# A two-layer decoder on one core: scatters of routed rows and fills of empty rows, moved to other slots of a written-out plan

## The chip, the cores and the metric

The kernel runs on one core of a Trainium2 chip, in float32. The time is the device time of one execution in microseconds; the median of several runs is compared. A separate execution, taken with the hardware profiler, gives the profile.

## The reference

The input x has 32 batch rows of 128 tokens with 128 features; a context has 32 rows of 128 tokens with 96 features, and a mask marks some of its tokens. Six residual blocks follow each other, each with a layer norm in front:

```python
x = x + rope_attention(ln(x))                    # 16 heads of 8
x = x + cross_attention(ln(x), ctx)              # 16 heads of 8
x = x + gated_moe(ln(x))                         # 8 experts, best 2, and 2 shared ones
x = x + causal_attention(ln(x))                  # 16 heads of 8, rotated q and k
x = x + latent_attention(ctx, ln(x), mask)       # 2 heads of 64, keys from ctx and x
x = x + relu_moe(ln(x))                          # 8 experts of width 512, best 2, biases
```

The last block matters most here. For each token it takes the softmax of eight router logits, keeps the two largest, divides them by their sum, and adds the two experts' outputs with these weights:

```python
probs = softmax(x @ router_w + router_b)
w, i = top_k(probs, 2); w = w / sum(w)
out = sum over the two: w * (relu(x @ w1[i] + b1[i]) @ w2[i] + b2[i])
```

## The kernel before

**Groups, slots and phases.** The 32 batch rows form 8 groups of 4. The kernel is one plan written by hand: `at(slot, phase, fn)` puts a function that issues instructions into a slot and a phase of it, and the slots are run through in order, so that each engine's queue has its instructions in the order of the plan. The phases that matter here are, in order, "open", "pre", (the attention's own work), "inner", "mid" and "post". The three attentions take 64 slots each (0–63 rope, 64–127 cross, 128–191 causal), two slots for each batch row; after slot 191 the plan goes on with latent attention, routing and experts. `done(stage, g)` is 8·(8·stage + g) + 17, the slot in which group g has left that attention; `done(2, 7)` is 201.

**Routing.** For the last block the groups are routed in five units, `UNITS = [(0, 1), (2, 3), (4, 5), (6,), (7,)]`: three pairs and two single groups. The units are collected into three parts, `UNITS_OF = [(0, 1), (2,), (3, 4)]`, so that groups 0–3, 4–5 and 6–7 go through the experts one part after the other. `plan_route` (from L1590) plans a unit: the norm's statistics (L1612, L1613 on DVE), its scale `r_rs` (L1618–L1621, on POOL), the normed rows (`rows`, L1629 on ACT, L1634 on POOL), the turned rows, logits (L1653), the choice of two experts, and then in one "mid" phase `ranks`: the gates' weights (`r_e`), a matmul that counts how many tokens before each chose the same expert (`ranks_pe`, L1701–L1703), and `places` (L1707–L1725). `places` is eleven small DVE instructions and two small POOL copies for a unit. It makes of the counts the row number at which each token goes into a buffer in DRAM (`r_ati`), the counts carried to the next unit (`carry`, L1713), and two extra columns of each row: the weight (L1724) and the token's number (L1725).

**Scatter.** Each expert has a region in the DRAM buffer `slots[f]` of its part f. `scatter(c, k)` (L1729) is one indirect DMA issued by POOL. It writes the 128 tokens of one batch row k, for their c-th choice, as rows of 130 floats (520 bytes) to the places in `r_ati`. A pair of groups has 16 such scatters, a single group 8: 64 in all. The plan places two per slot, one "pre" and one "inner", from the slot behind `ranks` on: a pair's 16 in 8 slots, a single group's 8 in 4 slots. The slots are 184–191, 200–207 and 216–223 for the pairs, and 222–225 and 230–233 for the single groups.

**Empty rows.** Rows of `slots` that no token goes to must hold something harmless. `preset(n)` (L2054–L2058) fills a quarter of one part's buffer with the row `nowhere`, whose token number is out of range, so that its result is not stored. There are 12 presets, issued by SP: four of 2210 KB and eight of 1170 KB, 18.2 MB. `once` (L2079) plans them in slots 4, 8, ... 48. The other loads and stores of these stages go through SP's queue too: the writes of `kv` (L1043, one per group), the copies of x to DRAM (`held`, L364), and for the first block of experts the gates' round trip through DRAM (`spread`, written at L918, read back by two DMAs per group as `g` at L921, which POOL waits for in `h`, L941).

**Experts.** `expert_blocks` (from L1818) works on blocks of 128 rows of `slots[f]`, two blocks (a pair) per slot. A part has 39, 23 and 23 blocks. For a pair: `fetch` loads two blocks of rows (`bx`, L1868, by SP, 20 buffers), `weights` copies the experts' weights (`w`, L1877 on ACT, L1879 on DVE), `turn` transposes the rows on PE (L1887, then `bxT` L1889 on DVE), `hidden` is the first product (L1897 on PE) with bias and relu (`bh`: L1903 on ACT, L1905 on DVE), `result` the second (L1914) with the gate's weight (`bo`: L1921 on ACT, L1923 on DVE), and `leave` stores each block's 128 results by an indirect DMA of POOL to the rows of `y` (L1928). So POOL issues two indirect DMAs per slot for the experts, and those of the scatters beside them. At the end `gather` and `finish` read `y` back and add it to x.

**When a part begins.** `beside` (from L1957) sets the slots in which the parts begin:

```python
begins = [done(2, 3) + 40]
begins.append(max(begins[0] + (NB[0] + 1) // 2, done(2, 5) + 40))
begins.append(max(begins[1] + (NB[1] + 1) // 2, done(2, 7) + 33))
```

These are 209, 229 and 241. A part's first four pairs are fetched in the "post" phase of that slot; its table of blocks is made four slots before. The first fetch of a part waits until all scatters into its buffer have landed.

Of the kernel before, what the change touches and what calls it, by code (L numbers as in the profile page):

```python
# [37 lines left out]
NB = [2 * r // BLOCK + E - 1 for r in ROOM]  # L38
# [75 lines left out]
def decoder(ctx: ExitStack, tc: tile.TileContext, a: dict, out: bass.AP):  # L114
# [132 lines left out]
    def wide(t, shape, axis):  # L247
        return t.unsqueeze(axis).to_broadcast(shape)
# [9 lines left out]
    def folded_bias(w_o, b_v, row, t):  # L258

        ps = bank(ps_m)  # L260
        nc.tensor.matmul(ps[:, :D], b_v.to_broadcast([D, P]), w_o, start=True, stop=True)
        nc.vector.tensor_tensor(t, ps[:, :D], row, ALU.add)
# [1304 lines left out]
    def store(g):  # L1567
        nc.sync.dma_start(out[g * NG : (g + 1) * NG].rearrange("b p d -> p b d"), X[g])
# [10 lines left out]
    def router(slots, lazy):  # L1579
# [8 lines left out]
        def plan_route(at, g, t):  # L1588
# [5 lines left out]
            groups = UNITS[q]  # L1594
# [5 lines left out]
            def tile8(tag, dtype=F32):  # L1600
                return small.tile([P, N2, E], dtype, tag="r8_" + tag, name="r8_" + tag, bufs=2)[:, :n2, :]
# [87 lines left out]
            def gates():  # L1689
                e, w = m["e"], col8("w")  # L1690
                nc.vector.tensor_tensor(e, e, m["both"], ALU.mult)
                nc.vector.tensor_reduce(w, e, AX.X, ALU.add)
                nc.vector.reciprocal(w, w)
                nc.vector.tensor_tensor(e, e, wide(w, [P, n2, E], 2), ALU.mult)
# [13 lines left out]
            def places():  # L1708
                place = tile8("place")
                nc.vector.tensor_tensor(  # L1710
                    place, m["rp"][:, : n2 * E].rearrange("p (b e) -> p b e", e=E), wide(before, [P, n2, E], 1), ALU.add
                )
                nc.vector.tensor_tensor(carry[q], m["rp"][:, n2 * E : (n2 + 1) * E], before, ALU.add)  # L1713
                at2 = small.tile([P, 2, N2], F32, tag="r_at", name="r_at", bufs=2)
                for c in range(2):
                    t = tile8("t")
                    nc.vector.tensor_tensor(t, m["picks"][:, c], place, ALU.mult)
                    nc.vector.tensor_reduce(at2[:, c, :n2], t, AX.X, ALU.add)
                m["ati"] = small.tile([P, 2, N2], I32, tag="r_ati", name="r_ati", bufs=2)
                nc.vector.tensor_copy(m["ati"][:, :, :n2], at2[:, :, :n2])  # L1720
                for c in range(2):
                    t = tile8("t")
                    nc.vector.tensor_tensor(t, m["picks"][:, c], m["e"], ALU.mult)
                    nc.vector.tensor_reduce(m["rows"][c][:, :n2, D + 1], t, AX.X, ALU.add)  # L1724
                    nc.gpsimd.tensor_copy(m["rows"][c][:, :n2, D].bitcast(I32), token[:, c, NG * groups[0] : NG * groups[0] + n2])  # L1725

            def scatter(c, n):
                def fn():
                    ins = nc.gpsimd.indirect_dma_start(  # L1729
                        slots[f], bass.IndirectOffsetOnAxis(ap=m["ati"][:, c, n : n + 1], axis=0), m["rows"][c][:, n, :], None,  # L1730
                        bounds_check=SLOTS[f] - 1, oob_is_err=False,
                    )
                    tc.declare_no_dep(ins.ins, group=f"slots{f}", reason="no two tokens have one slot")
                    tc.add_to_no_dep_group(f"slots{f}", ins.ins)
                return fn
# [34 lines left out]
            def ranks():  # L1770
                gates()
                ranks_pe()
                places()

            def gates_over(u):
                def fn():
# [27 lines left out]
            if len(groups) > 1:  # L1804
                t += 1
            at(t + 6, "mid", choose3)
            at(t + 7, "mid", ranks)
            n = 0
            for k in range(n2):
                for c in range(2):  # L1810
                    at(t + 8 + n // 2, ("pre", "inner")[n % 2], scatter(c, k))
                    n += 1
            for u in us:
                at(t + 8 + u, "mid", gates_over(u))
# [138 lines left out]
    def experts(halves, lazy, heads, late):  # L1953

        def beside(at, done):
            def swap():
                heads.close()  # L1957
                lazy["blocks"] = late.enter_context(tc.tile_pool(name="blocks", bufs=3, reuse_waits="tile"))

            def keep(e):  # L1960
                def fn():
                    rows = a["w_f"][e * P : (e + 1) * P]
                    if e == 0:
                        for tag, n in (("w1", W1), ("w2", 512)):
                            lazy[tag] = lazy["blocks"].tile([P, E * n], F32, tag=tag, name="all_" + tag, bufs=1)
                    nc.sync.dma_start(lazy["w1"][:, e * W1 : (e + 1) * W1], rows[:, :W1])
                    nc.sync.dma_start(lazy["w2"][:, e * 512 : (e + 1) * 512], rows[:, W1:])
                return fn

            at(done(2, G - 1) + 2, "open", swap)  # L1970
            for e in range(E):
                at(done(2, G - 1) + 2 + e, "open", keep(e))
            begins = [done(2, 3) + 40]
            begins.append(max(begins[0] + (NB[0] + 1) // 2, done(2, 5) + 40))
            begins.append(max(begins[1] + (NB[1] + 1) // 2, done(2, 7) + 33))

            def plan_part(f):
                table, fetch, weights, turn, hidden, result, leave, gather, finish = halves[f]
                t = begins[f]
                pairs = (NB[f] + 1) // 2  # L1980
                at(t - 4, "mid", table)
                for i in range(4):
                    at(t, "post", lambda i=i: fetch(i))
                for i in range(2):
                    at(t + i, "post", lambda i=i: weights(i))
                at(t + 1, "post", lambda: turn(0))
                for i in range(pairs):
                    s = t + 2 + i
                    if i + 1 < pairs:
                        at(s, "pre", lambda i=i: turn(i + 1))  # L1990
                    at(s, "inner", lambda i=i: hidden(i))
                    at(s + 1, "post", lambda i=i: result(i))
                    at(s + 2, "mid", lambda i=i: leave(i))
                    if i + 4 < pairs:
                        at(s, "post", lambda i=i: fetch(i + 4))
                    if i + 2 < pairs:
                        at(s, "post", lambda i=i: weights(i + 2))
                if f + 1 < len(PARTS):
                    for n, g in enumerate(PARTS[f]):
                        at(begins[f + 1] + 6 + 2 * n, "post", lambda g=g: gather(g))  # L2000
                        at(begins[f + 1] + 8 + 2 * n, "post", lambda g=g: finish(g))
                        at(begins[f + 1] + 10 + 2 * n, "post", lambda g=g: store(g))

            for f in range(len(PARTS)):
                plan_part(f)
        return beside
# [46 lines left out]
    def preset(n):  # L2053

        chunks = SLOTS[n // 4] // (2 * P)
        part = slots[n // 4].rearrange("(c p r) w -> p c (r w)", p=P, r=2)[:, n % 4 * chunks // 4 : (n % 4 + 1) * chunks // 4]
        nc.sync.dma_start(
            part, nowhere.rearrange("p r w -> p (r w)").unsqueeze(1).to_broadcast([P, chunks // 4, 2 * ROW])  # L2058
        )

    def once(at, done):

        at(-8, "mid", lambda: folded_bias(w_o0, b_v0, b_o0, bias0))
        at(8, "mid", lambda: nc.gpsimd.memset(z_all, 0.0))
        at(8, "mid", fold_context)
        at(9, "mid", fold_small)
        at(40, "mid", lambda: folded_bias(w_xo0, b_xv0, b_xo0, biasx))
        at(41, "mid", lambda: masked_bias(b_mx, b_xqk0[:, 0:1], b_xqk0[:, 1:2]))
        for n in range(2):
            at(104 + n, "mid", lambda n=n: fold_rotation(2 * n))  # L2070
        at(106, "mid", lambda: masked_bias(b_m1, b_qk1[:, 0:1], b_qk1[:, 2:3]))
        at(107, "mid", lambda: folded_bias(w_o1, b_v1, b_o1, bias1))
        at(108, "mid", lambda: folded_bias(w_xo1, b_vl, b_xo1, bias_l))
        for n in range(4 * len(PARTS)):
            at(4 + 4 * n, "mid", lambda n=n: preset(n))
        guard = []
        at(138, "mid", lambda: guard.append(cross_guard(word)))
        at(140, "mid", lambda: guard[0]())
# [125 lines left out]
```

## Time and profile before

| | before |
|---|---|
| runs | 1178.01, 1179.47, 1180.0 us |
| median | 1179.47 us |
| the profiled execution | 1184.79 us |
| its span in the profile | 1183.1 us |
| mean granted clock of TensorE | 0.943 |
| busy: PE / DVE / POOL / ACT | 1067.5 / 823.1 / 645.3 / 615.8 us |
| share of the chain that ended last: PE / DVE / POOL / ACT / DMA | 52 / 19 / 10 / 7 / 4% |
| 64 scatters L1729, busy on POOL | 63.6 us |
| 85 stores L1928, busy on POOL | 85.3 us |

How to read it: the engines are PE (matrix products), PEld (its weight loads), DVE, ACT, POOL and SP (which issues DMAs only). The profile cuts the span into 40 equal slices of 29.6 us and gives each engine's busy share in tenths, with a 9 for 90% or more; PEclk is the clock that PE was granted, in tenths. A group of instructions is a line such as "L1729 POOL DMA_INDIRECT slots<-rows,r_ati x64 | busy us, mean ns | idle before it, and what ended most of that idle time": the line of the kernel, the engine, the operation, what it writes and reads, and how often. "remote" and "issue" are names for idle time whose end no event in the trace explains. In a timeline, a bracket behind a row holds the idle time just before it and what ended it. The chain is the work that ended last, followed backwards from the last instruction to whatever released each step.

In the trace the experts' first rows (L1868) are loaded at 917 us and the last store of results (L1928) is issued at 1166 us.

### The profile page before, as it was taken

The numbers are of one execution on the slowest core, as the hardware profiler recorded it, in microseconds if no ns is written. First come the engines' busy times: TensorE is split into PE (matmuls) and PEld (weight loads), VectorE is DVE, ScalarE is ACT, GpSimd is POOL, SyncE is SP. The second block draws the span as 40 slices with busy tenths as digits, with TensorE's granted clock in tenths as the row PEclk, the third lists the DMA queues.
The fourth block names the chain that finished last, engine by engine and source line by source line (L and its number), as shares of the span: only waits on it lengthen the run. The fifth ranks groups of instructions, "written<-read, shape, count | busy, mean of one in ns | idle before, by whom it ended". The sixth has DMA issues, their size and how long they took to land.

```text
span 1183.1 us, 32419 instructions
## 1 busy us (share of the span) xinstructions
PE 1067.5 (90%) x12495; PEld 829.2 (70%) x12495; DVE 823.1 (70%) x2424; ACT 615.8 (52%) x1440; POOL 645.3 (55%) x918
## 2 busy tenths in 40 slices
PE   6999999999999999999998999989988888788893
PEld 3666667677767776677667677767766778678893
DVE  4678878878778666867787788778666565454652
ACT  2356555676655555554555666744633543333551
POOL 4576656434442544235647675746837245555653
PEclk9999989999999999999999999989976899888997
DMA  8753331000121011110110000001115222123432
GB/s 204 220 154 101 101 100 61 29 29 29 38 47 46 7 41 37 38 26 14 38 46 7 11 15 15 16 11 35 31 37 157 69 56 58 38 66 86 107 109 77
DMA packets 77858, 71.24 MB, mean 60 GB/s; under 512 B 14554, under 2 KB 66829, under 8 KB 77696
## 3 DMA queue, kind: packets, MB, share of 16 engines
q1 hardware_dynamic: 72640, 60.08, 18.7%
q0 software_dynamic: 4768, 8.47, 2.1%
q8 instruction: 102, 1.67, 0.6%
q10 hardware_dynamic: 288, 0.52, 0.1%
q14 instruction: 60, 0.49, 0.1%
HBM read 33.39 MB, written 37.02 MB: 60 GB/s over the span
## 4 chain that ended last, share of the span: by engine, by line
PE 52%; DVE 19%; POOL 10%; ACT 7%; issue 6%; DMA 4%; SPq 0%; another core or an unknown queue 0%; DVEq 0%; POOLq 0%; ACTq 0%
PE bank L633 11%; PE bank L1897 5%; PE bank L661 5%; PE bank L1914 5%; DVE msc L636 5%; PE bank L950 3%; DMA g<-spread 3%; POOL h L941 2%; ACT e L644 2%; PE bank L1121 2%; PE bank L511 1%; PE bank L932 1%; DVE qa L540 1%; PE bank L1200 1%; PE bank L1226 1%
## 5 line engine op out<-in xcount | busy, mean ns | idle before, releaser
L644 ACT ACTIVATE e<-bank 128x512 f32<-128x512 f32 x384 | 207.6, 593 | 178.5 <-PE bank L633 174.2
L636 DVE TENSOR_REDUCE msc<-bank 128x4 f32<-128x512 f32 x384 | 245.2, 680 | 70.1 <-PE bank L633 67.1
L633 PE MATMUL bank<-kb,qz 32*128 32x256 f32 x1536 | 243.8, 410 | 12.3 <-DVE msc L636 10.5
L633 PE MATMUL bank<-qa,kb 32*128 32x128 f32 x3072 | 235.9, 289 | 4.5 <-ACT e L644 4.5
L633 PEld LDWEIGHTS bank<-qa,kb 32*128 32x128 f32 x3072 | 196.6, 191 | 9.7 <-ACT e L644 8.8
L633 PEld LDWEIGHTS bank<-kb,qz 32*128 32x128 f32 x1536 | 146.8, 190 | 65.1 <-DVE msc L636 33.2
L1928 POOL DMA_INDIRECT y<-bo,bx x85 | 85.3, 1004 | 81.5 <-ACT bo L1921 44.0
L647 POOL TENSOR_SCALAR_AFFINE_SELECT e<-e 128x512 f32<-128x512 f32 x128 | 79.2, 642 | 69.5 <-ACT e L644 69.2
L661 PE MATMUL bank<-e,vt 128*32 128x128 f32 x3072 | 109.3, 284 | 0.5 <-POOL e L647 0.5
L1897 PE MATMUL bank<-bxT,w 128*128 128x128 f32 x680 | 92.1, 287 | 9.9 <-issue 9.4
L1897 PEld LDWEIGHTS bank<-bxT,w 128*128 128x128 f32 x680 | 85.9, 202 | 12.5 <-issue 12.0
L1914 PE MATMUL bank<-all_w,bh 128*128 x680 | 91.3, 289 | 3.6 <-issue 3.5
L661 PEld LDWEIGHTS bank<-e,vt 128*32 128x32 f32 x3072 | 81.5, 113 | 15.7 <-POOL e L647 1.5
L1914 PEld LDWEIGHTS bank<-all_w,bh 128*128 128x128 f32 x680 | 85.6, 204 | 6.0 <-issue 5.7
L1729 POOL DMA_INDIRECT slots<-rows,r_ati x64 | 63.6, 994 | 34.0 <-issue 18.4
L1905 DVE TENSOR_SCALAR bh<-bank,w 128x128 f32<-128x128 f32 x164 | 46.1, 343 | 43.8 <-remote 19.6
L941 POOL TENSOR_TENSOR h<-h,g 128x512 f32<-128x512 f32 x30 | 38.7, 1298 | 68.9 <-DMA g<-spread 58.3
L338 ACT ACTIVATE xn<-x,ln_nb,ln_rs 128x128 f32<-128x128 f32 x96 | 42.0, 492 | 49.9 <-POOL ln_nb L332 49.3
L1903 ACT ACTIVATE bh<-bank,w 128x128 f32<-128x128 f32 x176 | 50.3, 368 | 19.9 <-remote 7.7
L1207 ACT ACTIVATE le<-bank,lmx 128x256 f32<-128x256 f32 x64 | 26.9, 471 | 64.7 <-DVE lmx L1206 60.3
L540 DVE SCALAR_TENSOR_TENSOR qa<-bank,head_rows,qz 128x128 f32<-128x128 f32 x192 | 57.6, 342 | 0.0
L1921 ACT ACTIVATE bo<-bank,bx 128x128 f32<-128x128 f32 x44 | 16.2, 368 | 76.2 <-PE bank L1914 47.8
(337 smaller groups left out, 2320.5 us busy)
## 6 DMA issues: line engine op xcount, KB each, us to landing
slots<-nowhere SPq DMA_DIRECT2D x8, 1170.0 KB
slots<-nowhere SPq DMA_DIRECT2D x4, 2210.0 KB
g<-spread SPq DMA_DIRECT2D x16, 512.0 KB
bx<-slots SPq DMA_DIRECT2D x85, 65.0 KB
kv<-kcv SPq DMA_DIRECT2D x8, 516.0 KB
lkv<-kv SPq DMA_DIRECT2D x32, 129.0 KB
yg<-y SPq DMA_DIRECT2D x14, 256.0 KB
all_w<-in_w_f SPq DMA_DIRECT2D x8, 258.0 KB
```

The costliest lines, as they stand in the source:

```text
L540: nc.vector.scalar_tensor_tensor(s["qa"][:, u, :], s["mp"], head_rows[:, 1 - u : 2 - u], m["qz"][:, u, i * P : (i + 1) * P], ALU.mult, ALU.add
L633: nc.tensor.matmul(o, l, r, start=start, stop=stop, skip_group_check=True)
L636: nc.vector.tensor_reduce(tops(MSC[bb % 4], 2 * h + j), sc[j].rearrange("p (s n k) -> p s n k", s=2, n=2), AX.X, ALU.max, negate=True)
L644: nc.scalar.activation(e.rearrange("p n q -> p (n q)"), tr[j], AF.Exp, scale=SCALE)
L647: nc.gpsimd.affine_select(out=e, in_=e, compare_op=ALU.is_ge, fill=0.0, base=0, pattern=[[0, 4], [1, P]], channel_multiplier=-1)
L661: nc.tensor.matmul(s3["av"][32 * n : 32 * n + 32, h3 * P : (h3 + 1) * P], m3["vt"][:, i3, h3, n, u, :], es[u][:, n, :], start=(h3 == 0 and ...
L941: engine.tensor_tensor(m["h"][:, c, :], m["h"][:, c, :], m["g"][:, c, :], ALU.mult)
L1729: ins = nc.gpsimd.indirect_dma_start(slots[f], bass.IndirectOffsetOnAxis(ap=m["ati"][:, c, n : n + 1], axis=0), m["rows"][c][:, n, :], Non ...
L1897: nc.tensor.matmul(ps[:, c * P : (c + 1) * P], w[:, c * P : (c + 1) * P], s["xT"][:, u * P : (u + 1) * P], start=True, stop=True)
L1903: nc.scalar.activation(h, p, AF.Relu, bias=bias)
L1914: nc.tensor.matmul(ps[:, u * P : (u + 1) * P], s["h"][:, u, c, :], lazy["w2"][:, bass.ds(at_w + c * P, P)], start=(c == 0), stop=(c == 3),)
L1928: ins = nc.gpsimd.indirect_dma_start(y, bass.IndirectOffsetOnAxis(ap=x[:, D : D + 1].bitcast(U32), axis=0), s["o"][:, u, :], None, bounds_ ...
```

## The change

There are three edits, and a fourth that follows from them.

1. For a pair of groups, `places` is taken out of `ranks` and planned in the next slot's "pre" phase. The pair's 16 scatters begin one slot later, still two per slot: 185–192, 201–208 and 217–224. For a single group `places` stays where it is.
2. For a single group, the 8 scatters are planned one per slot, all in "pre": 222–229 and 230–237 instead of 222–225 and 230–233.
3. The 12 presets are planned in slots 20, 28, ... 108 ("post") instead of 4, 8, ... 48 ("mid").
4. In the third term of `begins`, 33 becomes 37. In both kernels the other term of that maximum is larger (229 + 12 = 241), so the parts begin in the same slots.

No instruction is added or removed.

```diff
             def ranks():
                 gates()
                 ranks_pe()
-                places()
+                if len(groups) == 1:
+                    places()
...
             at(t + 7, "mid", ranks)
+            if len(groups) > 1:
+                at(t + 8, "pre", places)
             n = 0
             for k in range(n2):
                 for c in range(2):
-                    at(t + 8 + n // 2, ("pre", "inner")[n % 2], scatter(c, k))
+                    if len(groups) > 1:
+                        at(t + 9 + n // 2, ("pre", "inner")[n % 2], scatter(c, k))
+                    else:
+                        at(t + 8 + n, "pre", scatter(c, k))
                     n += 1
...
-            begins.append(max(begins[1] + (NB[1] + 1) // 2, done(2, 7) + 33))
+            begins.append(max(begins[1] + (NB[1] + 1) // 2, done(2, 7) + 37))
...
         for n in range(4 * len(PARTS)):
-            at(4 + 4 * n, "mid", lambda n=n: preset(n))
+            at(20 + 8 * n, "post", lambda n=n: preset(n))
```

On the engines' queues this does the following. PE's and ACT's order is the same in both kernels. On DVE only the three pairs' `places` move: in units 0 and 1 behind the latent attention's copy `leT` (L1216), the norm statistics of another group (L1612, L1613) and the product `lqk` (L1122); in unit 2 behind `leT`, the statistics and the experts' `bo` (L1923) and `w` (L1879). On POOL the scatters move: in unit 1 two of them from behind `r_rs` to ahead of it, in unit 2 two from ahead of it to behind it, and the single groups' scatters from two behind each two `leave` stores to one. On SP the presets move: eight stand one by one among the writes of `kv` and the copies `held`, and the last four just before the copies `held` of the fourth to seventh groups, three of them right behind a group's two loads of `g`.

## The prediction, made before the changed kernel ran

> **What bounds the kernel.** I read the page's slices first (forty, each 29.6 us), then the chain of waits, then the timelines of PE and POOL in the last 240 us, where most of what the change moves lies.
>
> ```profile
> PE   6999999999999999999998999989988888788893
> POOL 4576656434442544235647675746837245555653
> PEclk9999989999999999999999999989976899888997
> DMA  8753331000121011110110000001115222123432
> ```
>
> PE is busy nine tenths up to 800 us and holds 52% of the chain. From slice 33 (976 us) on it sags to 8, with a 7 at slice 36 (1065 us), and in slices 31 to 36 the granted clock sags too. That stretch is the expert stage, where scatters of the last units (L1729) stand on POOL beside the expert blocks' leaving rows (L1928):
>
> ```profile
> L1928 POOL DMA_INDIRECT y<-bo,bx x85 | 85.3, 1004 | 81.5 <-ACT bo L1921 44.0
> L1729 POOL DMA_INDIRECT slots<-rows,r_ati x64 | 63.6, 994 | 34.0 <-issue 18.4
> L1905 DVE TENSOR_SCALAR bh<-bank,w 128x128 f32<-128x128 f32 x164 | 46.1, 343 | 43.8 <-remote 19.6
> ```
>
> An indirect DMA takes POOL 0.97 us and 0.30 us of issue behind it: 1.275 us back to back. The windows of ten (columns: busy us and count of PE, PEld, DVE, ACT, POOL, then granted clock, DMA share, GB/s) show what happens where POOL has many in a row:
>
> ```profile
> 1000.00:1010.00 10.00, 9.66 (x87) 9.29 (x87) 8.48 (x36) 6.06 (x16) 5.43 (x6) 1.00 0.23 57
> 1010.00:1020.00 10.00, 6.34 (x36) 4.63 (x35) 0.46 (x2) 1.14 (x4) 7.57 (x9) 0.90 0.18 53
> 1020.00:1030.00 10.00, 7.16 (x35) 6.20 (x36) 5.14 (x21) 2.70 (x8) 3.66 (x5) 0.59 0.07 22
> ```
>
> From 1006.88 to 1023.17 POOL issues 13 indirect DMAs without a break. Six microseconds in, PE falls from 87 matmuls per 10 us to 36, DVE and ACT nearly stop, and none of them names a releaser. The timelines of DVE, ACT and PE:
>
> ```profile
> 1019.78 1.12 DVE L1905 TENSOR_SCALAR bh<-bank,w 128x128 f32<-128x128 f32 x4 [9.54 <-remote]
> 1025.63 0.37 ACT L1921 ACTIVATE bo<-bank,bx 128x128 f32<-128x128 f32 x1 [9.72 <-remote]
> 1016.17 0.27 PE L1887 MATMUL bank<-ident,bx 128*128 128x128 f32 x1 [0.45 <-issue]
> ```
>
> PE then steps singly, one matmul per 0.72 us, until 1025.4. The same follows two more runs: 8 indirect DMAs with two copies (1031.6 to 1042.4: PE gaps of 4.6 us from 1037.7) and 10 (1060.1 to 1072.6: gaps of 2.73, 0.38 and 1.04 us, and ACT's bo 8.87 us late). Runs of 4 with a break of 1.8 us (988 to 1001) leave PE 96% busy, and runs of 2 (1084 to 1150) leave it full at 3.79 us per pair of blocks. So I read: **a run of indirect DMAs longer than about 6 us stalls the other engines until one or two microseconds after its end.** From 1000 to 1084 us PE finishes 12 pairs; at 3.79 us, with 5.7 us of other PE work there, that is 51.2 us, and with the clock's sag it took 79: some 28 us are at stake.
>
> **The change, part by part.** I made the sum against the profiled execution's own 1184.8 us (span 1183.1); the median of the runs is 1179.5, 5.3 less, and I take the difference over unchanged. In the built programs PE and ACT keep their order; the pairs' places move on DVE, and scatters and presets move on POOL and SP.
>
> *Presets* (the empty rows, twelve DMAs on SP). They start at 41 us before, five in a row, and at about 96 us after, one per eight slots, the last at some 415 us:
>
> ```profile
> slots<-nowhere SPq DMA_DIRECT2D x8, 1170.0 KB
> slots<-nowhere SPq DMA_DIRECT2D x4, 2210.0 KB
> ```
>
> Before, they flood the DMA engines (slices 1 to 4), yet a group of the first attention takes 28.45 us under the flood (48.38 to 76.83) and 28.45 us after it (88.73 to 117.18): nothing to win. After, each goes ahead of a write of kv (first read at 619 us), ahead of a held copy, or behind the two loads of g (groups 0 to 2). POOL's h waits for g (58.3 us in all), but on SP the preset stands behind those loads; a held copy of 256 KB already follows there, and the waits with and without one are alike (6.99 to 8.40 us). Cost 0; the bound above is a third of a preset's transfer at the 220 GB/s of slice 1 (5.3 us / 3) on each of three groups, about +6; below 0.
>
> *Pairs.* The places are eleven small DVE instructions, 2.1 us (876.0 to 878.0 in unit 1). A slot later they stand behind leT, lqk and the norm's sums, which PE waits for: 0.66 and 0.79 us at 796 and 798 us (unit 0), 0.82 and 0.76 us near 880 (unit 1). Half of each is gained: −0.7 and −0.8; ends 0 and −1.5 each. What is late next are the scatters, one slot: in unit 1, two of them (2.55 us) move ahead of POOL's r_rs, which ACT's rows (L1629) and PE's L1641 already wait for (1.07 and 0.99 us): +1.3, ends 0 and +2.2. In unit 2, two scatters move from ahead of r_rs to behind it, so the four-long run at 965.6, with ACT's rgT 3.57 us late, starts earlier: −1.5, ends 0 and −4. Sum −1.7.
>
> *Single groups.* Scatters go from two per slot in 222–225 and 230–233 to one in 222–229 and 230–237. In slots 222–223, where unit 2's pair scatters overlap (and, after, 224), POOL's list turns from "y y s s s s" to "y y s s s". By the rows' times that makes the 13-run a 12-run: −1.3. Behind r_rs the list was y y s s, copy, y y, copy, y y; it becomes y y s, copy, y y s, copy, y y s: nine instead of eight: +1.3. The 10-run at 1060 (s s y y s s y y s s) becomes s y y s y y s y y, eight or nine, and the stall behind it halves (8.3 us by the ACT and PE waits, PE's half of it counted): −3.5. The scatters moved out of it go to slots 234–237 with three indirect DMAs each: POOL 3.83 us per slot against PE's 3.79: +1.2, ends +0.2 and +5. Sum −2.3. The lower end: POOL holds 45 indirect DMAs between 1001.4 and 1084, 57.4 us, with 4 us of copies and small operations; if nothing stalls, 61.4 instead of 82.8: −21.
>
> *Part 1's first load* waits on SP for the last scatter of unit 3, before at 1035.7 with the load at 1037.4; PE wants it at 1061.1. After, that scatter sits at slot 229, about 1052.4 by the y y of 1049.9 ahead of it. It lands 2.1 us later (a piece of the chain shows 2.11), and the load needs about 2.8: 1057.3. Cover shrinks from 20 us to 4. Cost 0; +3 if POOL lags. Queued behind that load on SP are only the next loads. The start slots of the parts stay 209, 229 and 241 (33 to 37 is covered by the larger term).
>
> Sum: 0 − 1.7 − 2.3 + 0 = **−4.0 us: 1180.8 by the profile, 1175.5 by the median.**
>
> A rule that speaks against the spreading: the Trainium skill, "SBUF — State Buffer" (the "DVE blocks DMA" trap), says a DMA issued from GpSimd waits for its descriptors while DVE copies fp32 within SBUF, 620 ns becoming about 3100 ns. DVE's weight copy L1879 is such a copy, one per slot, and single scatters would meet more of them: eight of those waits would cost some 20 us, an estimate from that page. The trace disagrees: all 64 scatters lie between 966 and 1237 ns, at most 0.27 us over the shortest, and here DVE is the one that waits; by these rows the term is under 2 us.
>
> **Rivals.**
> *A, forecast: runs get shorter* (0.44): 1165 to 1177, point 1175.5. For it: breaks of 1.8 us suffice at 988–1001. Against: the three-per-slot stretch has hardly a break.
> *B, an even trade* (0.20): scatters per run fall, the number of runs rises, or the stalls come from something the change doesn't move (the clock sags too, but behind each stall). 1177.1 to 1181.9, point 1179.5.
> *C, slower* (0.36): three per slot keep POOL continuous in 222–237, since PE's 3.79 us leaves no break below 3.83. It decides from where PE needs less than 3.83 us per slot. Then the stalled state lasts: in the 8.5 us behind 1066 PE lost 4.15, about 0.4 of the time per us with the singles; over slots 233–237 (19 us, 6 free) +5.2; POOL lags and part 1's load is late, +3; the −3.5 does not come; pairs −1.7: +6.5, point 1186, to 1191.
> *D, the edit does nothing*: only the 33-to-37 edit; the rest moves instructions, so D is inside B.
>
> **Numbers.** (0.2%, 2.4 us, is about what a measurement can tell here.) Faster 0.44, same 0.20, slower 0.36. All bounds together reach from −28 (−21 − 1.5 − 1.5 − 4) to +17.5 (6 + 2.2 + 1.3 + 5 + 3); the range cuts one in ten off each side, ending in A below and in C above: 1165 to 1188. A's own range is 1165 to 1177.
>
> **What would show it.** In the profile after: groups of the first attention still 28.45 us; presets from 96 us on; POOL's run near 1006 of 12 and the one near 1060 of 8 or 9; "remote" waits of DVE's bh under 19.6 us and ACT's bo likewise; PE's L1887 near 1061 with no wait for bx. Wrong if the remote waits stay with runs of three, if bx is named there with over 1 us, or if g's waits grow past 9 us.

## The result, and the profile after

The change made the kernel slower: 1184.28 us (median of 20 runs, 1175.36 to 1190.36) against 1179.37 us before (20 runs, 1174.05 to 1182.90). The ratio is 1.0043, with an interval of 1.0026 to 1.0060: +5.1 us, between +3.1 and +7.1. A gain of 4.0 us to 1175.5 was forecast.

The profiled execution of the changed kernel took 1175.36 us, the shortest of its 20 runs, with a span of 1173.7 us. It is thus 9.4 us below the span of before's profile although the kernel is slower: totals of single profiles mislead here, and what follows reads single waits, and stretches of the run between two fixed instructions. The page's rows that answer to those of before:

```profile
PE   6999999999999999999998999989988898878993
POOL 4576666434442544235647675756838245656663
PEclk9889989999999999999999999999996798799997
DMA  8303331222233031100110000001115222123432
...
L1934 POOL DMA_INDIRECT y<-bo,bx x85 | 85.3, 1003 | 78.3 <-ACT bo L1927 42.3
...
L1911 DVE TENSOR_SCALAR bh<-bank,w 128x128 f32<-128x128 f32 x164 | 46.0, 342 | 50.3 <-remote 28.3
...
L1729 POOL DMA_INDIRECT slots<-rows,r_ati x64 | 63.4, 991 | 22.1 <-issue 21.6
```

The presets now fill the DMA slices 4 to 15 instead of 1 to 4, and the first attention doesn't notice: the group that begins at 88.73 us in before takes 28.45 us there and 28.44 in the changed kernel. (Lines behind the edits moved by up to six: L1928 is now L1934, L1905 is L1911, L1887 is L1893.) The long run of POOL near 1000 us is still there, with the same picture on PE, DVE and ACT. The windows of ten (columns as in the prediction):

```profile
990.00:1000.00 10.00, 9.93 (x91) 9.52 (x90) 8.79 (x41) 4.98 (x14) 5.74 (x8) 1.00 0.22 56
1000.00:1010.00 10.00, 7.11 (x47) 6.29 (x46) 1.43 (x4) 2.13 (x6) 7.56 (x8) 0.82 0.18 54
1010.00:1020.00 10.00, 7.85 (x32) 6.94 (x32) 5.42 (x20) 2.03 (x6) 3.76 (x7) 0.50 0.07 22
```

POOL issues 12 indirect DMAs from 997.76 to 1012.78 where 13 were, as forecast. The run near 1060 has 7 (8 or 9 were forecast). DVE's bh still waits for a "remote" event, 28.3 us in all where 19.6 were:

```profile
1013.33 1.12 DVE L1911 TENSOR_SCALAR bh<-bank,w 128x128 f32<-128x128 f32 x4 [10.19 <-remote]
```

A place where the change costs time is earlier, on POOL, where the scatters of unit 1 stand. Before, from POOL's timeline:

```profile
878.50 1.12 POOL L1729 DMA_INDIRECT slots<-rows,r_ati  x1 [6.30 <-DVE rows L1724]
879.92 0.98 POOL L1729 DMA_INDIRECT slots<-rows,r_ati  x1 [0.30 <-issue]
887.72 1.68 POOL L1139 TENSOR_TENSOR nrml<-nrml,half 128x8 f32<-128x8 f32 x1 [6.82 <-DVE nrml L997]
...
914.65 0.97 POOL L1729 DMA_INDIRECT slots<-rows,r_ati  x1 [0.30 <-issue]
915.69 0.25 POOL L1618 TENSOR_SCALAR r_rs<-r_mv 128x8 f32<-128x8 f32 x1
```

And after:

```profile
878.05 1.67 POOL L1139 TENSOR_TENSOR nrml<-nrml,half 128x8 f32<-128x8 f32 x1 [13.50 <-DVE nrml L997]
879.90 1.12 POOL L1729 DMA_INDIRECT slots<-rows,r_ati  x1 [0.18 <-POOL nrml L1139]
...
906.85 0.97 POOL L1729 DMA_INDIRECT slots<-rows,r_ati  x1 [0.30 <-issue]
907.89 0.25 POOL L1618 TENSOR_SCALAR r_rs<-r_mv 128x8 f32<-128x8 f32 x1
```

nrml (L1139) is a scale of the causal attention, and r_rs is that of unit 2's routing. POOL waits some 13 us for nrml in both. Before, the unit's first two scatters were done inside that idle time; after, they stand behind nrml, in a stretch in which POOL is nearly full until r_rs: 16 scatters instead of 14. From nrml to r_rs it is 28.0 us before and 29.8 after (before had 0.87 us of idle time in it). r_rs makes the normed rows that PE's L1641 turns. PE's waits there, before and after (total, how often, longest, from 780 to 1060 us):

```profile
PE bank L1641 <- ACT rows L1629: 2.1, 2, 1.1
```
```profile
PE bank L1641 <- ACT rows L1629: 5.0, 3, 2.5
```

ACT's order is the same in both kernels, so a stretch can be cut at the same two ACT instructions in each profile. The stretch that runs from 905 to 925 us in before took 21.1 us before and 24.1 after. The mean granted clock in it was 0.74 before and 0.64 after, so this pair of profiles alone doesn't tell how much of the 3.0 us is r_rs.

### The profile page after: what moved, and what is told of

It reads as the page before. It is cut to its first block, busy times and chain, and to the rows that moved or that the text cites. A ratio compares the mean times of both kernels' runs of the same rounds, so it can differ in the third digit from the quotient of the medians.

```text
span 1173.7 us, 32413 instructions
## 1 busy us (share of the span) xinstructions
PE 1059.6 (90%) x12495; PEld 825.9 (70%) x12495; DVE 821.6 (70%) x2424; ACT 614.8 (52%) x1440; POOL 646.6 (55%) x918
## 3 DMA queue, kind: packets, MB, share of 16 engines
q1 hardware_dynamic: 72640, 60.08, 18.8%
## 4 chain that ended last, share of the span: by engine, by line
PE 57%; DVE 15%; POOL 9%; ACT 7%; issue 6%; DMA 3%; SPq 1%; another core or an unknown queue 0%; POOLq 0%; DVEq 0%; ACTq 0%
PE bank L633 13%; PE bank L1920 7%; PE bank L1903 6%; PE bank L661 6%; DVE msc L636 4%; PE bank L950 3%; POOL h L941 2%; DMA g<-spread 2%; PE bank L932 2%; ACT e L644 2%; PE bank L933 2%; PE bank L1121 1%; PE bank L486 1%; PE bank L511 1%; POOL slots L1729 1%
## 5 line engine op out<-in xcount | busy, mean ns | idle before, releaser
L1934 POOL DMA_INDIRECT y<-bo,bx x85 | 85.3, 1003 | 78.3 <-ACT bo L1927 42.3
L647 POOL TENSOR_SCALAR_AFFINE_SELECT e<-e 128x512 f32<-128x512 f32 x128 | 79.5, 646 | 69.7 <-ACT e L644 69.1
L661 PE MATMUL bank<-e,vt 128*32 128x128 f32 x3072 | 109.2, 283 | 0.8 <-POOL e L647 0.5
L661 PEld LDWEIGHTS bank<-e,vt 128*32 128x32 f32 x3072 | 80.9, 112 | 16.0 <-issue 2.7
L1911 DVE TENSOR_SCALAR bh<-bank,w 128x128 f32<-128x128 f32 x164 | 46.0, 342 | 50.3 <-remote 28.3
L1729 POOL DMA_INDIRECT slots<-rows,r_ati x64 | 63.4, 991 | 22.1 <-issue 21.6
L1927 ACT ACTIVATE bo<-bank,bx 128x128 f32<-128x128 f32 x44 | 16.1, 368 | 72.9 <-PE bank L1920 35.4
```

The source lines that it names most:

```text
L647: nc.gpsimd.affine_select(out=e, in_=e, compare_op=ALU.is_ge, fill=0.0, base=0, pattern=[[0, 4], [1, P]], channel_multiplier=-1)
L661: nc.tensor.matmul(s3["av"][32 * n : 32 * n + 32, h3 * P : (h3 + 1) * P], m3["vt"][:, i3, h3, n, u, :], es[u][:, n, :], start=(h3 == 0 and ...
L1729: ins = nc.gpsimd.indirect_dma_start(slots[f], bass.IndirectOffsetOnAxis(ap=m["ati"][:, c, n : n + 1], axis=0), m["rows"][c][:, n, :], Non ...
L1934: ins = nc.gpsimd.indirect_dma_start(y, bass.IndirectOffsetOnAxis(ap=x[:, D : D + 1].bitcast(U32), axis=0), s["o"][:, u, :], None, bounds_ ...
```

## The experiments

**Two kinds of chips.** Each set of experiments ran on one chip, each on another. The kernel before took about 1147 us in three sets and 1180 in two. In the twelve profiles of the first kind no wait ends with "remote"; in the profiles of the second kind these waits stand (65.9 us in all engines in before's), as in the profiles of the result. Each experiment is compared with runs of before on its own chip, in microseconds worked out from the ratio; I call the kinds quiet (1147) and stalling (1180). No chip was used in two sets of experiments, so whether the kind belongs to the chip or to the time of the runs isn't shown.

The first set took the change apart, on a quiet chip. Theory: three indirect DMAs per slot keep POOL continuous (rival C). Rivals: the presets; the pairs.

*e1, presets alone:* `at(20 + 8 * n, "post", ...)` for `at(4 + 4 * n, "mid", ...)`.

> The kernel before with the presets alone moved to slots 20 to 108. If the later presets carry the loss (they stand among the writes of kv and the loads of g), this kernel is 4 to 6 us slower than before, and POOL's waits for g grow past 9 us a group. If the loss is in the expert stage or in the clock, it is within 2 us of before, and the whole first 900 us keep their times but for the clock.

1147.07 us, ratio 0.9992 (0.9967 to 1.0016). The presets cost nothing that shows.

*e2, pairs alone:*

```diff
-                places()
+                if len(groups) == 1:
+                    places()
...
+            if len(groups) > 1:
+                at(t + 8, "pre", places)
...
-                    at(t + 8 + n // 2, ("pre", "inner")[n % 2], scatter(c, k))
+                    if len(groups) > 1:
+                        at(t + 9 + n // 2, ("pre", "inner")[n % 2], scatter(c, k))
```

> The kernel before with the pairs alone changed: their places one slot behind the counts, their scatters one slot later. By the prediction's terms -1.7 us (between -7 and +2). If the loss is here, +4 to +6 us, to be seen near 796, 880 or 960 us.

1152.74 us, ratio 1.0046 (1.0025 to 1.0067): +5.3 us. The loss is here, and the -1.7 us of the prediction has the wrong sign.

*e3, single groups alone:* `at(t + 8 + n, "pre", scatter(c, k))` for them, and 37 for 33.

> The kernel before with the single groups' scatters alone at one per slot (and 37 for 33). By the prediction's terms -2.3 us. By the rival with three indirect DMAs per slot that keep POOL continuous, +4 to +8 us, with the waits called remote of bh and bo longer in sum than the 46 us of before (19.6 + 18.6 + 7.7).

1146.22 us, ratio 1.0006 (0.9978 to 1.0034). No loss that shows: rival C fails on this chip, where no remote waits are.

*e4, the changed kernel again:*

> The changed kernel once more, unaltered, for a second profile and for its clock. If its times fall in two groups (near 1175 and near 1185) because of the granted clock alone, the times follow the clock with some 6 us per 0.01. If a stall in the expert stage comes and goes, the second profile shows the remote waits grow by 5 to 10 us against the first (28.3 us of DVE's bh, 11.9 of ACT's bo, 12.9 of ACT's bh).

1148.74 us, ratio 1.0021 (0.9990 to 1.0051). No remote waits at all, against both expectations: they don't belong to the kernel alone. Its times still spread from 1143 to 1159.

The second set took the pairs apart, on another quiet chip.

*f1, places late, scatters not:* e2 with `t + 8` for `t + 9`.

> The kernel before with the pairs' places one slot later, and their scatters where they were (the first two right behind the places). If the pair's loss (+5.3 us for both) comes from the scatters that pass POOL's next r_rs, this is within 1 us of before or up to 1.5 us faster (leT and lqk early). If it comes from the places beside other DVE work, it is 3 to 5 us slower.

1147.34 us, ratio 0.9977 (0.9961 to 0.9993): 2.6 us faster. Of the waits that e1 has on PE, L502's for leT (1.2) and L1121's for carry (0.6) are gone, L1226's for leT falls from 1.8 to 0.4, and of 0.8 for lv 0.3 is left.

*f2, scatters late, places not:* the reverse.

> The kernel before with the pairs' scatters one slot later, and their places where they were. By the r_rs theory +4 to +6 us, with PE's L1641 waiting some 3 us for ACT's rows in unit 2 instead of 1.4. By the places theory within 1 us of before.

1156.20 us, ratio 1.0057 (1.0035 to 1.0080): +6.5 us. The shift of the scatters carries the loss. PE's waits from 780 to 1060 us in f2, and one of f1:

```profile
PE bank L1641 <- ACT rows L1629: 9.9, 5, 4.4
...
PE bank L661 <- POOL e L647: 1.4, 3, 0.6
```
```profile
PE bank L1641 <- ACT rows L1629: 6.1, 4, 3.2
```

In e1 they were 5.1 (1.8 at the longest) and 0.2 us. The stretches cut at the same ACT instructions (named by their times in before's profile; us) show three places:

| stretch | e1, e3 | places late (f1, h5) | scatters late (f2) | pairs (e2, h2) | changed kernel (e4, h3) | f4 |
|---|---|---|---|---|---|---|
| 840–860 | 19.9, 19.9 | 19.9, 19.9 | 22.2 | 21.0, 21.1 | 22.1, 22.1 | 19.9 |
| 905–925 | 21.7, 20.6 | 22.5, 20.5 | 24.7 | 24.3, 24.4 | 24.4, 24.3 | 20.5 |
| 925–940 | 13.7, 14.8 | 13.3, 16.4 | 13.6 | 13.7, 13.4 | 13.5, 13.6 | 23.3 |
| 1030–1050 | 18.8, 13.8 | 21.3, 21.8 | 22.2 | 21.9, 22.0 | 17.9, 16.1 | 22.4 |

All three late places are an r_rs behind the scatters of the unit before: the r_rs of unit 1 (behind unit 0's scatters, where the causal mask's select L647 is late too), that of unit 2 (behind unit 1's), and that of unit 4 (behind unit 2's). For unit 2's r_rs POOL's timelines show it: from nrml to r_rs it is 27.3 to 28.2 us where unit 1's scatters stand as in before or where f4 puts two of them behind, and 29.8 to 30.5 where all 16 are a slot late (seventeen profiles; g4, k1 and k2, with six scatters first, left out).

The last row is less plain. It is also late in f1 and h5 (21.3 and 21.8, with L1641 waiting 3.2 and 3.5 us there, 1.8 in e1), whose scatters keep their slots: r_rs starts at 1010.1 us in e1 and in f1, behind the same row of indirect DMAs, and PE only comes to it earlier. So there late places alone lose most of what late scatters lose. Single groups at one per slot (e3) put 51 scatters ahead of that r_rs instead of 54 and win 4 to 6 us in this row, partly in half-speed pieces of PE's clock. In e3 and h1 2.7 us of them are lost again behind 1095 us, and their times show next to no gain; still it fits that the whole change loses less than the pairs alone. A piece of 3.4 us at half clock costs up to 1.7 us, and such pieces blur single cells of the last three rows; in the row 840–860 the clock was full in every profile.

*f3, the pair edit in unit 1 alone:* the conditions read `q == 1`.

> The pair edit in unit 1 (groups 2 and 3) alone. By the r_rs theory about +2 us: +3 in the 25 us in which unit 2's rows are normed and turned, less 1 from leT and lqk just before. If the loss sits in unit 0 or 2, within 1 us of before.

1149.24 us, ratio 0.9998 (0.9973 to 1.0022): inconclusive, the expected +2 lies inside the interval, and so does nothing. Its profile has the L1641 wait (3.7 us at the longest).

*f4, r_rs first:* the last two scatters of unit 1 in "post" of their slot, those of unit 0 three slots later.

> The pair edit as a whole, but the last two scatters of units 0 and 1 put behind the next unit's r_rs. By the r_rs theory the loss goes: between -1.5 and +1 us against before, L1641 waiting about 1.4 us at most. If the loss does not hang on r_rs, +3 to +5 us stay.

1153.34 us, ratio 1.0034 (1.0012 to 1.0057): +3.9 us stay, which reads as a refutation, but the table shows the rows 840–860 and 905–925 back at 19.9 and 20.5, and a new 23.3 in 925–940 (part of it a lower granted clock, 0.64 against 0.75 in e1). There the first load of part 0 waits for the last scatter, which the edit had put later still. PE in f4:

```profile
PE bank L1894 <- DVE bxT L1896: 8.6, 2, 7.0
...
PE bank L1894 <- DMA bx<-slots: 3.4, 2, 3.0
```

So the late r_rs of units 1 and 2 was mended as the theory says, and the wait moved to the load. That of unit 4 stayed late (22.4), since f4 leaves unit 2's scatters a slot late.

The third set fell on a stalling chip.

*g1 and g2, scatters late in unit 1 alone, in unit 0 alone:*

> The kernel before with the scatters of unit 1 alone one slot later, the places untouched. If the loss comes from two scatters that leave POOL's idle stretch ahead of nrml (6.8 us) for the full stretch ahead of r_rs: PE's L1641 waits 3 to 3.7 us instead of 1.1 for its first rows, +2.5 to +3.5 us in all. If it comes from unit 0 or 2: within 1 us.

> The same for unit 0 alone. By that theory +1 to +2.5 us: r_rs of unit 1 1.3 us later, the causal mask's select L647 behind it, PE's L661 waiting 0.8 to 1.4 us instead of 0.2. If unit 2 holds the rest of the 7.5 us that shifting all three pairs' scatters costs at equal clock: within 1 us.

1181.83 us, ratio 1.0026 (0.9996 to 1.0055), and 1183.29 us, 1.0011 (0.9982 to 1.0039). Neither is clear of zero by itself, but the profiles show each effect in its own place only: the stretch 905–925 is 24.5 us in g1 and 21.1 in g2, 840–860 is 19.9 in g1 and 22.2 in g2. The granted clock in 905–925 is 0.77 in g1, 0.74 in g2 and 0.74 in before, so here the 3.4 us are not the clock's. PE in g1, with one wait of 3.4 us where before had 1.1:

```profile
PE bank L1641 <- ACT rows L1629: 6.2, 3, 3.4
```

*g3, the changed kernel with the pairs' scatters put back a slot; g4, places late, single groups one per slot, and six scatters of unit 1 first:* in g4 `at(t + 8 + (max(0, n - 4) if q == 1 else n) // 2, ...)`.

> The changed kernel with its pairs' scatters put back a slot, all else as in it (places late, single groups one per slot, presets late). If the shift of the scatters is the whole loss: 0 to 5 us faster than before. If the changed kernel's loss is also in the presets or the single groups: 1 to 4 us slower than before.

> The kernel before with the pairs' places a slot later, the single groups' scatters one per slot, and the first six scatters of unit 1 together in POOL's idle stretch ahead of nrml. If r_rs behind the scatters is what costs, turning the move round gains: L1641's waits fall under 1 us in unit 2 and in unit 4, 3 to 6 us faster than before. If not: within 1.5 us of it.

1181.89 us, ratio 1.0021 (0.9999 to 1.0042), and 1185.80 us, ratio 1.0028 (1.0000 to 1.0056). g3 lies in the branch of its expectation that puts a loss into the presets or the single groups too, though its interval reaches to zero, and g4, which was to be 3 to 6 us faster, missed. On this kind of chip something else in them costs.

The fourth set (quiet again) repeats the parts side by side: *h1* is e3, *h2* is e2, *h3* is the changed kernel, *h5* is f1.

> Single groups at one per slot alone. Where before's profile has no remote waits: within 2 us of before, the two waits of L1641 in unit 4 (1.8 and 0.8 us) gone. Where it has them: if three indirect DMAs per slot prolong them, +2 to +5 us; if shorter runs shorten them, -2 to -5 us.

> The pair edit alone: +4 to +6 us if the loss is that of POOL's queue ahead of r_rs, wherever it runs; within 2 us of before where remote waits stand, if those swallow it.

> The whole change: the sum of pairs and single groups in the same call, within 2 us.

> Places a slot late, scatters where they were: 1 to 3 us faster than before on any chip, since PE's waits for leT, lv and the carry (0.7 to 0.8 us each, 2 to 3 us in all) go and POOL's queue ahead of r_rs is as before.

h1 1145.01 us, 0.9989 (0.9967 to 1.0012); h2 1150.51 us, 1.0028 (1.0006 to 1.0049); h3 1148.97 us, 1.0021 (0.9997 to 1.0045); h5 1147.65 us, 0.9999 (0.9973 to 1.0026). h1 and h3 came as expected; h2, at +3.2 us, fell short of its 4 to 6, and h5 missed its gain of 1 to 3. The means of the first and the fourth set: pairs +4.2 us, single groups -0.3, sum with the presets (-0.9, measured once) +3.0; the whole +2.4. The parts add up within their intervals.

The last set, on a stalling chip: *k1* is g4 again, *k2* is k1 with the places left in `ranks` for all units, so single groups one per slot and six scatters first.

> Places late, single groups one per slot, six of unit 1's scatters first. Without remote waits: 2 to 5 us faster than before, L1641 under 1 us in unit 2. With them (before near 1180): 0 to 5 us slower, as g4.

> The kernel before with single groups one per slot and six of unit 1's scatters first, places as before. Without remote waits: 2 to 4 us faster than before. If the front-loading does nothing, the 1 us of the single groups alone.

k1 1187.40 us, ratio 1.0038 (1.0012 to 1.0064); k2 1179.03 us, ratio 0.9988 (0.9964 to 1.0013). k1 came as expected for this kind of chip; for k2 only a gain without remote waits had been named. They differ in the places alone, and by 8.4 us in the median (5.9 by the ratios). In unit 2 of k1 POOL runs from 961.49 to 982.11 without a break of half a microsecond, 14 indirect DMAs and 6 small operations; in k2 a wait of 2.34 us for rows cuts this into 6 and 8. Behind k1's run PE stands idle:

```profile
975.55 0.39 PE L1226 MATMUL bank<-lkv,leT 128*128 128x65 f32 x2
984.57 0.26 PE L1195 MATMUL bank<-masked,ident_b 32*128 32x128 bf16 x1 [8.62 <-ACT rT L1647]
```

The stretch 960–985 is 29.1 us in k1, 28.4 and 28.5 in g4 and g3, and 22.4 in k2; with the order of before it is 26.2 in before and 22.5 and 22.9 in g1 and g2. So on stalling chips late places with unmoved scatters join two runs into one, and the engines wait longer there. That this makes k1 slower isn't shown: from 960 to 1095 us the two profiles differ by 1.7 us only (136.7 and 135.0). The changed kernel, whose scatters move too, has runs of 7 and 9 there and 20.5 us.

No version was found that is clearly faster than the kernel before on both kinds; f1 was on one quiet chip (and level on another), k2 is level on a stalling one.

## Why the prediction was wrong

**The presets cost nothing:** right (e1, on a quiet chip). The sign of 9 us for g's waits was taken from pieces of the chain (6.99 to 8.40 us); POOL's longest wait for g is 12.3 us in before already, and 11.9 in e1. The upper bound of +6 is, by its own terms (5.3 us / 3 on three groups), 5.3. **The start of part 1:** right; in the changed kernel's profiles PE's first turns of part 1 wait for no load. **Places late save leT, lv and the carry:** the waits go, as forecast; -1.5 us was forecast for two units, f1 measured -2.6 and h5 -0.1.

**The step that failed is the pairs' "What is late next are the scatters, one slot".** It was priced for unit 1 alone, at +1.3 us (0 to +2.2), and nothing was put down for unit 0; for unit 2 the same shift was counted as a gain of 1.5. Measured on quiet chips: +1.1 to +2.3 in unit 0 (r_rs, and the select behind it, which PE's L661 waits for), about +3 in unit 1, and for unit 2 about +3 at unit 4's r_rs as long as the single groups are two per slot, of which late places alone bring most. The pairs' sum was -1.7 and measured +5.3 and +3.2.

The error behind it: the prediction, and the section on the change, has two scatters of unit 1 pass from behind r_rs to ahead of it. None does: 32 scatters stand ahead of unit 2's r_rs in both traces. What changes is where they stand. Two of them leave POOL's idle stretch (13 us, ahead of nrml) for one that is nearly full up to r_rs, so that almost their whole 2.55 us, and not half, arrive on PE: L1641's longest wait there is 1.1 to 1.4 us without the shift and 3.3 to 3.7 with it (2.5 in the profile of the result). The same happens in unit 0, for which nothing was put down.

Unit 2's gain, forecast at -1.5, does show in the profile of the result: ACT's rgT no longer waits 3.57 us for a remote event, and the stretch 960–985 is 20.5 us instead of 26.2. On quiet chips there is no such wait to save, and no run on a stalling chip has this edit alone.

**The single groups' -2.3 us** rested on runs of indirect DMAs longer than 6 us stalling the other engines. That the 13-run would be 12, and the run behind r_rs nine, came true to the count. But the rule, read off one profile, fails on quiet chips: there the changed kernel's POOL has a run of 76 indirect DMAs and 17 other operations from 959 to 1064 us without a break of 0.6 us, and PE goes on beside it (windows of 20 us of h3):

```profile
960.00:980.00 20.00, 19.70 (x167) 18.18 (x166) 12.24 (x38) 10.96 (x31) 15.58 (x19) 1.00 0.25 62
980.00:1000.00 20.00, 19.91 (x177) 19.15 (x176) 15.95 (x66) 9.65 (x26) 15.20 (x17) 1.00 0.29 72
```

On quiet chips there was thus nothing for the -2.3 to save. On a stalling chip this edit wasn't run alone; in the profile of the result all engines' remote waits are some 8 us shorter than in before, though bh's grew. The same two windows in k1, on a stalling chip:

```profile
960.00:980.00 20.00, 14.55 (x114) 12.56 (x114) 8.57 (x30) 7.32 (x21) 14.83 (x19) 0.89 0.19 51
980.00:1000.00 20.00, 14.69 (x110) 13.50 (x110) 8.88 (x31) 5.82 (x16) 7.71 (x9) 0.76 0.16 38
```

**Rival C**, slower by POOL's continuity with three DMAs per slot, had the sign and nearly the size (+6.5) but, as far as is shown, not the cause: e3 and h1 show no loss from it on quiet chips, and k2, which has three per slot on a stalling one, is level. **The Trainium skill's** "DVE blocks DMA" rule ("SBUF — State Buffer") would have added some 20 us, by the prediction's estimate from that page. The trace disagrees: the 64 scatters after still average 991 ns, and the five of them that run beside a copy of w on DVE (L1879, now L1885) take 977 ns at most.

**What stays open:** the cause is shown on quiet chips, where the whole change costs 2.4 us. On stalling chips, where the result was measured, g1 and g2 show the late r_rs in its place (3.4 and 2.3 us of stretch), but their times aren't clear of zero, the profile of the result has only 0.4 us of it in unit 0's stretch, and presets, single groups and the pairs as a whole weren't measured alone. So how the +5.1 us divide there is not assigned. And what makes a chip stall was not found.

## What to carry to other kernels

A step that is moved on an in-order queue is priced by the idle time that it leaves and the full stretch that it enters: look up the engine's next real wait on both sides, and follow what stands behind it to the bottleneck. When an edit undoes one wait, look for the next consumer before calling the theory dead: f4 mended two waits and made a third. And a stall whose releaser the profile can't name may go with the chip, or with the time of the runs, and not with the kernel alone, so a gain that rests on it should be small in the sum.

## What the runs showed of the hardware

The same kernel takes 1147 us on three chips and 1180 on others. The stretch from 960 to 1095 us, cut at the same ACT instructions, is 134.7 us in before's profile, at a mean granted clock of 0.89, and 104.1 at 0.98 in e1's on a quiet chip: 30.6 of the 32 us. POOL's indirect DMA takes 0.97 us on both kinds; what the stalling chips have more of are waits of the other engines that end with no event in the trace.

PE's clock falls to half in pieces of about 3.4 us, or a multiple. Some stand at the same place in several profiles (near 629, 666 and 789 us in before's and in e1's), others don't. One began where PE had been busy without a gap: in e1's profile PE is busy for all of the 10 us ahead of 932.5, and the clock is 0.51 in the 3.4 us behind it. Over the runs of the kernel before, the time goes with the mean granted clock, 5 to 8 us per 0.01 in each set. That is more than this change: the twelve runs of e4 alone spread over 16 us.
